# Attention over 3327 nodes on one core: query blocks of 512 instead of 476, with the remainders of two groups in one block

## The chip, the cores and the metric

The kernel runs on one core of a Trainium2 chip. The metric is the device time in microseconds (us); lower is better. Three runs of the kernel before gave a median of 9959.76 us (9959.03 to 9964.47). The profile shows one execution of the same kernel.

## The reference, cut to what matters

Two graph layers over N = 3327 nodes of 128 features. The first is a small graph attention with softmax over neighbours. The second is the expensive one: for each of d = 128 "heads" it forms a full N x N score matrix from only 8 values per node, adds the adjacency matrix twice, takes a softmax over all N keys, and multiplies with 8 values per key.

```
q = (x @ Wq.T).reshape(d, n, h)          # d = 128, n = 3327, h = 8
k = (x @ Wk.T).reshape(d, n, h)
v = (x @ Wv.T).reshape(d, n, h)
a = jnp.einsum('dnh,dmh->dnm', q, k) * scale
a = a + spatial_encoding + edge_encoding # both are the 0/1 adjacency matrix
a = jax.nn.softmax(a, axis=2)
out = jnp.einsum('dnm,dmh->dnh', a, v)
out = out.reshape(n, h * d) @ Wo.T
x = _layernorm(x + out)
```

That is 128 x 3327 x 3327, or 1.4 billion, exponentials, and as many additions or multiplications for the adjacency.

## The kernel before, in words

**Tiles.** Scores are laid out with keys in the partitions and queries along the free axis. The 3327 keys make 26 tiles of 127 or 128 keys. The 128 heads are taken in 32 groups of four (`HG = 4`, `NG = 32`). Within a group the queries are cut into `NBLK = 7` blocks: six of `WB = 476` and one of 472 (`exact`, lines 101 and 102). So there are 32 x 7 = 224 blocks, each of 26 key tiles by four heads by 476 queries.

**Per key tile.** `pair_scores` (the matmul of line 152) computes the scores of one head from 32 rows: the four heads of a group lie in the four row groups of TensorE, so they can run together. Two heads share a PSUM tile `scb` of two banks. The adjacency enters in one of two ways:

- "times": ScalarE takes the exponential of two heads from PSUM to SBUF (line 1194), then GpSimd multiplies by a factor of 1 or e squared per pair of nodes (line 1195). The factor is made once per block position by `make_factor` and kept in DRAM (`ftd`).
- "adds": VectorE adds the adjacency while it moves two heads from PSUM to SBUF (line 1197). One step later ScalarE takes the exponential of all four heads in place (line 1004, `exp_late`).

`plans` says which key tile goes which way, so that all engines are loaded: of three key tiles one is multiplied and two are added. An even-numbered and an odd-numbered block have slightly different plans. `laid` turns a plan into 26 rounds (`NR`); the rounds hold 18 or 17 exponentials of line 1194, and on average 17.5 of each kind.

**Products.** `products` (line 961) multiplies the finished exponentials `e4` with the values `v4`, which have nine columns (eight values and a one, whose sum is the softmax's divisor) in a 32-column slot. The four heads use the four column groups of TensorE, and all accumulate into one PSUM bank `av`, in the order head 0, 1, 2, 3. A product of this kind in float32 is two weight loads and two matmuls in the profile. `LAG` holds the products about five rounds behind the scores. After the last key tile, VectorE copies `av` to `o4` (line 971), which goes to DRAM (`oT`).

**Loads.** `want_adj` loads adjacency and factors three stretches ahead on SP's queue, `open_queries` the next block's queries, `open_group` the keys and values of the next group. A group is opened `OPEN` = 18 rounds before its first block, and `finish_to` forces whatever rows of the first layer it needs that are not yet done.

**Side work.** Everything else is threaded through these rounds by hand: the first layer's rows (`layer0`), their projections to q, k and v (`project`, `high`, `low`, `values`), the counts that check the input's form, and the output rows (`result`). `lane(kind, n, odd)` says in which rounds a unit of side work may go: "p" and "q" are matmuls, "d" and "l" VectorE, "m" GpSimd. Split values `hi` and `lo` (lines 396 to 425) gather 512 columns before they are stored.

**Order.** The program orders every engine's instructions by hand (`manual_schedule`); the loops of lines 1149 to 1209 write them: group, block, round.

Of the kernel before, what the change touches and what calls it, by code (L numbers as in the profile page):

```python
# [47 lines left out]
def kernel(  # L48
# [52 lines left out]
    LW = -(-(N - (NBLK - 1) * WB) // 2) * 2  # L101
    exact = [(b * WB, 0, WB) for b in range(NBLK - 1)] + [(N - LW, (NBLK - 1) * WB - N + LW, LW)]

# [20 lines left out]
    ftd = [dram.tile([NP, P, WB], F32, name=f"ftd{b}") for b in range(NBLK)]  # L124
# [25 lines left out]
    def special():  # L150
# [9 lines left out]
        with ExitStack() as sx, tc.manual_schedule(engines=ALL):  # L160
# [30 lines left out]

            ones = keep.tile([P, 1], F32, name="ones")
# [74 lines left out]
            def layer0(t, side=True, trow=None, bank=bank, held=None):  # L267
# [128 lines left out]
                def high(c, scale):  # L396
                    if c % 512 == 0:
                        s["hi"] = bg2.tile([P, 512], F32R, name="hi")
                        s["lo"] = bg2.tile([P, 512], F32R, name="lo")
                    o, hi = c % 512, s["hi"]  # L400
                    if side:
                        nc.vector.tensor_scalar(hi[:r, o : o + QW], s["b"][:r, :QW], scale, None, op0=ALU.mult)  # L402
                    else:
                        nc.scalar.mul(hi[:r, o : o + QW], s["b"][:r, :QW], scale)

                def low(dst, c, scale):
                    o = c % 512
                    hi, lo = s["hi"], s["lo"]
                    nc.vector.scalar_tensor_tensor(  # L409
                        lo[:r, o : o + QW], s["b"][:r, :QW], scale, hi[:r, o : o + QW].bitcast(F32),  # L410
                        op0=ALU.mult, op1=ALU.subtract,
                    )
                    if o + QW == 512:
                        h0 = c // 512 * 4
                        for half, sb in ((0, hi), (1, lo)):
                            at = (h0 * 2 + half if dst is qT else half * H + h0) * G + t * P * D
                            for p0, p1 in _cut(r):
                                later = held.append if held is not None and dst is qT else issue
                                engine = nc.sync if later is issue else nc.scalar
                                later(  # L420
                                    lambda at=at, sb=sb, p0=p0, p1=p1, engine=engine: engine.dma_start(
                                        _ap(dst, at + p0 * D, [[D, p1 - p0], [2 * G if dst is qT else G, 4], [1, D]]),
                                        sb[p0:p1].bitcast(F32).rearrange("p (h c) -> p h c", c=D),
                                    )
                                )

# [304 lines left out]
            def open_queries(g, b):  # L731
                q4 = qp.tile([P, WB], F32R, name="q4b")
                n0, _, w = exact[b]

                def head(j, engine=nc.sync):
                    for again in range(2):
                        engine.dma_start(
                            q4[32 * j + 16 * again : 32 * j + 16 * again + 16, :w].bitcast(F32),
                            _ap(qT, (g * HG + j) * N + n0, [[G, 2 * H], [1, w]]),
                        )  # L740

                return q4, head


            def kind(g, b):

                return (g * NBLK + b) % 2

            stretches = [
                (g, b, m) for g in range(NG) for b in range(NBLK) for m in range(len(plans[kind(g, b)]))  # L750
            ]
# [3 lines left out]
            def want_adj(n):  # L755
# [3 lines left out]
                g, b, m = stretches[n]  # L759
                a = adjs[n] = ap_.tile([P, 3, WB], F32, name="at")  # L760
                n0, _, w = exact[b]
                times, adds = plans[kind(g, b)][m]
# [26 lines left out]
            def make_factor(n):  # L789
                if n < len(stretches):  # L790
                    g, b, m = stretches[n]
                    times, _ = plans[kind(g, b)][m]
# [11 lines left out]
            with ExitStack() as st:  # L804
# [21 lines left out]
                first = layer0(0, side=False, trow=t0, bank=next_bank, held=held)  # L826
# [128 lines left out]
            def products(s, i):  # L955
                if s.left == NT:
                    s.av = pv.tile([P, WB], F32, name="av")
                r, e = kr[i], s.e.pop(i)
                s.left -= 1
                for j in range(HG):  # L960
                    nc.tensor.matmul(  # L961
                        s.av[32 * j : 32 * j + 32, : s.w],
                        s.v4[:r, j, i * H1 : i * H1 + 32],
                        e[:r, j, : s.w],
                        start=(s.left == NT - 1),
                        stop=(s.left == 0),
                    )
                if s.left == 0:
                    o4 = op_.tile([P, WB], F32, name="o4")
                    n0, c0, w = exact[s.b]  # L970
                    nc.vector.tensor_copy(o4[:, :w], s.av[:, :w])  # L971
                    for j in range(HG):
                        d = s.g * HG + j
                        issue(
                            lambda engine=nc.sync, j=j, d=d: engine.dma_start(
                                oT[:, d * N + n0 + c0 : d * N + n0 + w], o4[32 * j : 32 * j + H1, c0:w]
                            )
                        )
# [20 lines left out]
            def exp_late(now):  # L999
                for item in [x for x in late if x[0] <= now]:  # L1000
                    late.remove(item)
                    _, s, i, h0, h1 = item
                    e = s.e[i][: kr[i], h0:h1, : s.w]
                    nc.scalar.activation(e, e, AF.Exp, scale=2.0)  # L1004
# [6 lines left out]
            total = NBLK * NR  # L1011

            OPEN = min(18, total // 2)
# [6 lines left out]
            def lane(kind, n, odd):  # L1020

                n -= odd
                if n == NR - 2 and odd:
                    return int(kind != "l")
# [4 lines left out]
                return int(n % 3 == {"q": 0, "l": 2}.get(kind, 1) or n % 3 == 1 and kind == "q")  # L1029
# [25 lines left out]
            results = [((needs[t] + 1) * total + LAG + 6, result(t)) for t in range(NT - 1)]  # L1055
# [5 lines left out]
            def head(row, now, force=False):  # L1061

                while True:
                    if not side[row]:
                        if row != "main":
                            return None
                        ahead = ("rows", reads[min(max(now, 0) // total + 2, NG - 1)]) in marks
# [26 lines left out]
            def work_tensor(now, n, odd):  # L1094

                kind = head("main", now)
                if kind in ("p", "q") and lane(kind, n, odd) and side["read"] != now - 1:
                    run("main", now)

            def work(now, n, odd):  # L1100
                room, low, pool = lane("d", n, odd), lane("l", n, odd), lane("m", n, odd)
# [28 lines left out]
            queries = open_queries(0, 0)  # L1130
# [18 lines left out]
            for g in range(NG):  # L1149
                k4, v4, _ = group  # L1150
                for b in range(NBLK):
                    s = Block()
                    s.g, s.b, s.q4, s.k4, s.v4, s.left, s.e, added = g, b, queries[0], k4, v4, NT, {}, {}
                    w = s.w = exact[b][2]
                    odd = kind(g, b)
                    rounds, order, starts = plan_of[odd]
                    for n, rnd in enumerate(rounds):
                        at = b * NR + n
                        if n in starts:
                            m = number[g, b, starts[n]]  # L1160
                            if m:
                                want_adj(m + AHEAD)
                            a = adjs[m]
                        tick()
                        if n % 5 == 4 and first_loads:
                            first_loads.pop(0)[1]()
                        if g + 1 < NG:
                            if at == total - OPEN:
                                finish_to(("rows", reads[g + 1]), None)
                                tick(True)  # L1170
                                group = open_group(g + 1)
                            for k, f in enumerate(group[2]):
                                if at >= total - OPEN and at == total - OPEN + OPEN * k // len(group[2]):
                                    f()
                        if n == NR // 2 and (b + 1 < NBLK or g + 1 < NG):
                            queries = open_queries(g, b + 1) if b + 1 < NBLK else open_queries(g + 1, 0)
                        for j in range(HG):
                            if n == NR // 2 + j * (NR > 12) and (b + 1 < NBLK or g + 1 < NG):
                                queries[1](j)
                        sc = {}  # L1180
# [415 lines left out]
```

## Time and profile before

| | us |
| --- | --- |
| median of three runs | 9959.76 |
| profiled execution, whole | 9959.44 |
| its span, first to last instruction | 9957.7 |
| first exponential of line 1194 | 54.2 |
| start of the last exponential of line 1004 | 9931.2 |

The granted TensorE clock averaged 0.996 of full speed. The DMA engines were busy for some 60% of the time and moved 1755.28 MB, 176 GB/s on average.

A line of the costliest groups reads: line of the code, engine, operation, tile written and tiles read, partitions x elements, count; then busy time in total, mean nanoseconds of one; then the idle time of the engine just before such instructions, and what ended most of it. In the waits, the columns are total time, number of waits and the longest. In a timeline, they are start, duration, engine, line, operation and count. Instructions on one engine overlap: a duration runs from the start of an instruction until it is done, while the next one may start before that.

### The profile page before, as it was taken

Reading aid. Unit: us, or ns where it says so; the run is one execution under the profiler, and the core shown is the slowest. Engines: PE = TensorE matmul, PEld = TensorE weight load, DVE = VectorE, ACT = ScalarE, POOL = GpSimd, SP = SyncE. Lnnn points to the kernel's source line nnn. Section 1 sums busy time; section 2 is a strip of 40 time slices with the busy share of each in tenths; the row PEclk is TensorE's granted clock in tenths of the full one; section 3 lists DMA queues with packets and bytes.
Section 4 is the critical chain, followed back from the end, with each engine's and each line's share of the span. In section 5 each row is a group of like instructions: output and inputs, shape, how many; then the busy total and the mean of one; then the engine's idle time right before and its main releaser. Section 6 shows DMA issues by size and latency. Waiting matters only on the chain.

```text
span 9957.7 us, 207593 instructions
## 1 busy us (share of the span) xinstructions
PE 9447.6 (95%) x79523; PEld 3001.3 (30%) x79523; DVE 9210.8 (92%) x10585; ACT 9859.0 (99%) x7904; POOL 9158.9 (92%) x4923
## 2 busy tenths in 40 slices
PE   8999999999999999999999999999999999999998
PEld 3233233333233333333233333333333232222222
DVE  8999999999999999999999999999999998888888
ACT  7999999999999999999999999999999999999998
POOL 7999999999899999999999999999999998888887
PEclk9999999999999999999999999999999999999999
DMA  6666556656665656656556566566665665555554
GB/s 202 206 184 181 180 172 183 183 170 185 175 180 171 183 169 186 188 168 181 177 174 186 173 182 178 170 180 181 185 180 168 178 175 164 164 157 168 164 166 133
DMA packets 1399670, 1755.28 MB, mean 176 GB/s; under 512 B 349488, under 2 KB 1387018, under 8 KB 1394568
## 3 DMA queue, kind: packets, MB, share of 16 engines
q1 hardware_dynamic: 1395328, 1740.03, 59.4%
q8 instruction: 626, 10.26, 0.4%
q14 instruction: 380, 3.11, 0.1%
q10 hardware_dynamic: 3336, 1.88, 0.1%
HBM read 1637.49 MB, written 103.93 MB: 175 GB/s over the span
## 4 chain that ended last, share of the span: by engine, by line
ACT 44%; PE 30%; issue 10%; POOL 8%; DVE 5%; DMA 1%; SPq 0%; POOLq 0%; DVEq 0%; ACTq 0%
ACT e L1004 32%; PE av L961 15%; PE scb L152 12%; ACT e L1194 12%; POOL e L1195 7%; DVE e L1197 4%; PE bank L241 2%; DVE o L971 1%; DMA at<-in_adjT_dram 0%; POOL w L308 0%; POOL w L317 0%; DMA at<-ftd 0%; DVE dump L326 0%; DVE lo L409 0%; DMA q4b<-qT 0%
## 5 line engine op out<-in xcount | busy, mean ns | idle before, releaser
L1195 POOL TENSOR_TENSOR e<-e,at 128x952 f32<-128x952 f32 (+1 forms) x3920 | 8719.1, 2240 | 745.5 <-ACT e L1194 683.3
L1197 DVE TENSOR_TENSOR e<-scb,at 128x952 f32<-128x952 f32 (+1 forms) x7728 | 8497.2, 1141 | 681.8 <-PE scb L152 488.8
L1004 ACT ACTIVATE e<-e 128x1904 f32<-128x1904 f32 (+3 forms) x3920 | 7477.3, 1908 | 12.2 <-DVE e L1197 11.5
L961 PE MATMUL av<-e,v4b 128*32 128x476 f32 (+1 forms) x46592 | 5817.5, 572 | 44.1 <-DVE o L971 35.5
L1194 ACT ACTIVATE e<-scb 128x952 f32<-128x952 f32 (+1 forms) x3920 | 4300.2, 1097 | 35.7 <-PE scb L152 18.0
L152 PE MATMUL scb<-q4b,k4b 32*128 32x476 f32 (+1 forms) x23296 | 3861.7, 485 | 431.8 <-ACT e L1194 295.9
L152 PEld LDWEIGHTS scb<-q4b,k4b 32*128 32x128 f32 (+1 forms) x23296 | 1750.7, 189 | 5410.9 <-ACT e L1194 3210.5
L961 PEld LDWEIGHTS av<-e,v4b 128*32 128x32 f32 (+1 forms) x46592 | 1031.9, 108 | 1206.1 <-issue 1018.3
L241 PE MATMUL bank<-hsb,w 128*32 128x129 f32 (+1 forms) x5200 | 278.2, 286 | 0.0
L326 DVE TENSOR_SCALAR_CACHE_REDUCE dump<-a 128x384 bf16<-128x384 f32 (+2 forms) x468 | 247.0, 528 | 0.6
L308 POOL TENSOR_SCALAR w<-trow,er 128x129 f32<-128x129 f32 x650 | 233.8, 386 | 1.1
L317 POOL TENSOR_TENSOR w<-w,a 128x384 f32<-128x384 f32 (+3 forms) x225 | 210.1, 934 | 0.1
L241 PEld LDWEIGHTS bank<-hsb,w 128*32 128x32 f32 (+1 forms) x5200 | 102.4, 108 | 148.3 <-issue 148.3
L971 DVE COPY o<-av 128x476 f32<-128x476 f32 (+1 forms) x224 | 143.8, 642 | 3.4 <-PE av L961 3.4
L241 PE MATMUL bank<-wo,ot 128*32 128x128 f32 x1600 | 85.2, 285 | 0.0
L409 DVE SCALAR_TENSOR_TENSOR lo<-bank,hi 128x256 fp32r<-128x256 f32 (+1 forms) x200 | 82.6, 413 | 0.0
L402 DVE TENSOR_SCALAR hi<-bank 128x256 fp32r<-128x256 f32 (+1 forms) x200 | 82.4, 412 | 0.0
L241 PE MATMUL bank<-wk,x1T 128*32 128x256 f32 x800 | 63.9, 391 | 0.0
L241 PE MATMUL bank<-wv,x1T 128*32 128x256 f32 x800 | 63.9, 391 | 0.0
L241 PE MATMUL bank<-wq,x1T 128*32 128x256 f32 x800 | 63.9, 391 | 0.0
L503 PE MATMUL bank<-ident,o 128*128 128x128 f32 x225 | 52.0, 304 | 0.0
L241 PEld LDWEIGHTS bank<-wo,ot 128*32 128x32 f32 x1600 | 31.5, 108 | 45.6 <-issue 45.6
(124 smaller groups left out, 636.4 us busy)
## 6 DMA issues: line engine op xcount, KB each, us to landing
at<-in_adjT_dram SPq DMA_DIRECT2D x1536, 476.0 KB
at<-ftd SPq DMA_DIRECT2D x1674, 238.0 KB
at<-in_adjT_dram SPq DMA_DIRECT2D x256, 472.0 KB
at<-ftd SPq DMA_DIRECT2D x279, 236.0 KB
k4b<-kT SPq DMA_DIRECT2D x124, 415.9 KB
q4b<-qT SPq DMA_DIRECT2D x1536, 29.8 KB
at<-in_adjT_dram SPq DMA_DIRECT2D x192, 208.2 KB
at<-in_adjT_dram SPq DMA_DIRECT2D x150, 238.0 KB
```

Of the source, the lines that this page charges most:

```text
L152: nc.tensor.matmul(dst, k4[32 * j : 32 * j + H4, first_key(i) : first_key(i) + 2 * r - 1 : 2], q4[32 * j : 32 * j + H4, :nb], start=True, ...
L241: nc.tensor.matmul(dst[c0:c1], w[:, c0:c1], mov, **kw)
L308: nc.gpsimd.tensor_scalar(w, s["t"][:, :, :T3], -LOWEST, e, op0=ALU.min, op1=ALU.max)
L317: nc.gpsimd.tensor_tensor(w, w, s["a"][n][:, c0 - i0 : c1 - i0, :r], op=ALU.mult)
L326: nc.vector.tensor_scalar(z, a, float(k), None, op0=ALU.is_equal, op1=ALU.add, accum_out=even[:, t, at : at + 1])
L409: nc.vector.scalar_tensor_tensor(lo[:r, o : o + QW], s["b"][:r, :QW], scale, hi[:r, o : o + QW].bitcast(F32), op0=ALU.mult, op1=ALU.subtract,)
L961: nc.tensor.matmul(s.av[32 * j : 32 * j + 32, : s.w], s.v4[:r, j, i * H1 : i * H1 + 32], e[:r, j, : s.w], start=(s.left == NT - 1), stop=( ...
L971: nc.vector.tensor_copy(o4[:, :w], s.av[:, :w])
L1004: nc.scalar.activation(e, e, AF.Exp, scale=2.0)
L1194: nc.scalar.activation(eh, z[:r, :, :w], AF.Exp, scale=2.0)
L1195: nc.gpsimd.tensor_tensor(eh, eh, ah, op=ALU.mult)
L1197: nc.vector.tensor_tensor(eh, z[:r, :, :w], ah, op=ALU.add)
```

## The change

Blocks become 512 queries wide. 3327 = 6 x 512 + 255, so a group has six full blocks and a remainder of 256 (one query is computed twice). The remainders of two neighbouring groups are put side by side in one block of 512: its first half belongs to the even group, its second half to the odd one. A pair of groups thus has 13 blocks (six, the shared one, six), and the whole 208 instead of 224. In a shared block each score matmul and each product is split into two of 256 columns, since the two halves have different keys and values; exponentials, additions and multiplications cover both halves in one instruction. The adjacency of the remainder is loaded once for two groups.

Around this:

- [...] a shared block first writes zeros with one product against `nought`, and then only accumulates.
- A group whose first block comes early is opened earlier: `begins` holds the round at which a group starts (an odd group in the shared block), and group 1 is opened 10 rounds ahead, not 18.
- `lane` lets no side matmuls into shared blocks, gives "q" every round from the sixth on instead of two of three, and gives VectorE's "d" a further round of three until group 1 has begun.
- `hi` and `lo` become tiles of one projection's width (256 columns in side work), each stored on its own; the prologue gets four of them from a pool of its own.

```diff
-    LW = -(-(N - (NBLK - 1) * WB) // 2) * 2
-    exact = [(b * WB, 0, WB) for b in range(NBLK - 1)] + [(N - LW, (NBLK - 1) * WB - N + LW, LW)]
+    W = 512
+    NF = N // W
+    HALF = -(-(N - NF * W) // 2) * 2
+    exact = [(b * W, 0, W) for b in range(NF)] + [(N - HALF, NF * W - N + HALF, HALF)]
...
+            sequence = []
+            for g in range(0, NG, 2):
+                sequence += [([g], b) for b in range(NF)] + [([g, g + 1], NF)] + [([g + 1], b) for b in range(NF)]
...
+                if s.left == NT - 1 and len(s.v4) > 1:
+                    for j in range(HG):
+                        nc.tensor.matmul(s.av[32 * j : 32 * j + 32, :], nought[:r], e[:r, j, :], start=True, stop=False)
                 for j in range(HG):
-                    nc.tensor.matmul(
-                        s.av[32 * j : 32 * j + 32, : s.w],
-                        s.v4[:r, j, i * H1 : i * H1 + 32],
-                        e[:r, j, : s.w],
-                        start=(s.left == NT - 1),
-                        stop=(s.left == 0),
-                    )
+                    for k, v4 in enumerate(s.v4):
+                        nc.tensor.matmul(
+                            s.av[32 * j : 32 * j + 32, k * w : k * w + w],
+                            v4[:r, j, i * H1 : i * H1 + 32],
+                            e[:r, j, k * w : k * w + w],
+                            start=(s.left == NT - 1 and len(s.v4) == 1),
+                            stop=(s.left == 0 and k + 1 == len(s.v4)),
+                        )
...
-            OPEN = min(18, total // 2)
+            begins = [(g // 2 * 13 + g % 2 * NF) * NR for g in range(NG)]
+            OPEN = [0, 10] + [18] * (NG - 2)
...
-            def lane(kind, n, odd):
+            def lane(kind, n, odd, both):
+                if both and kind in "pq":
+                    return 0
                 n -= odd
+                if kind == "d" and opening == 1 and n > 6 and n % 3 == 2:
+                    return 1
...
-                return int(n % 3 == {"q": 0, "l": 2}.get(kind, 1) or n % 3 == 1 and kind == "q")
+                return int(kind == "q" or n % 3 == (2 if kind == "l" else 1))
...
+                        for k, k4 in enumerate(s.k4):
+                            c = slice(k * w, k * w + w)
                             for t in range(2):
-                                pair_scores(sc[i, h][: kr[i], t, :w], s.k4, s.q4, i, kr[i], 2 * h + t, w)
+                                pair_scores(sc[i, h][: kr[i], t, c], k4, s.q4[:, c], i, kr[i], 2 * h + t, w)
...
-                            ah = a[:r, at_ or 0, :w].unsqueeze(1).to_broadcast([r, 2, w])
+                        ah = a[:r, at_ or 0, :w].unsqueeze(1).to_broadcast([r, W // w * 2, w])
```

## The prediction

> **What bounds the kernel now.** I read the engine shares first, then the costliest groups, then the waits, then ScalarE's timeline start by start.
>
> ```profile
> PE 9447.6 (95%) x79523; PEld 3001.3 (30%) x79523; DVE 9210.8 (92%) x10585; ACT 9859.0 (99%) x7904; POOL 9158.9 (92%) x4923
> ...
> L1195 POOL TENSOR_TENSOR e<-e,at 128x952 f32<-128x952 f32 (+1 forms) x3920 | 8719.1, 2240 | 745.5 <-ACT e L1194 683.3
> L1197 DVE TENSOR_TENSOR e<-scb,at 128x952 f32<-128x952 f32 (+1 forms) x7728 | 8497.2, 1141 | 681.8 <-PE scb L152 488.8
> L1004 ACT ACTIVATE e<-e 128x1904 f32<-128x1904 f32 (+3 forms) x3920 | 7477.3, 1908 | 12.2 <-DVE e L1197 11.5
> ...
> L1194 ACT ACTIVATE e<-scb 128x952 f32<-128x952 f32 (+1 forms) x3920 | 4300.2, 1097 | 35.7 <-PE scb L152 18.0
> ```
>
> ScalarE is busy 99% of the span, and its two exponentials stood idle 12.2 and 35.7 us in all. VectorE and GpSimd have 7 to 8% free. The waits say the same from the other side:
>
> ```profile
> PEld scb L152 <- ACT e L1194: 3210.5, 3587, 1.5
> ...
> POOL e L1195 <- ACT e L1194: 683.3, 2284, 7.1
> ...
> ACT e L1194 <- PE scb L152: 18.0, 14, 4.0
> ...
> ACT e L1004 <- DVE e L1197: 11.5, 15, 3.1
> ```
>
> The others wait for ScalarE (TensorE 3,587 times); ScalarE waits 14 and 15 times. So ScalarE's time per instruction, start to start, is what a change must alter:
>
> ```profile
> 5014.39 1.08 ACT L1194 ACTIVATE e<-scb 128x952 f32<-128x952 f32 x1
> 5015.23 1.92 ACT L1004 ACTIVATE e<-e 128x1904 f32<-128x1904 f32 x1
> 5016.91 1.08 ACT L1194 ACTIVATE e<-scb 128x952 f32<-128x952 f32 x1
> ...
> 5093.80 1.07 ACT L1004 ACTIVATE e<-e 128x952 f32<-128x952 f32 x1
> 5094.69 1.03 ACT L1194 ACTIVATE e<-scb 128x952 f32<-128x952 f32 x1
> ```
>
> The second number, a duration, contains queueing; the differences of the first do not. L1194 over 952 elements holds the engine 0.84 us, L1004 over 1904 holds it 1.68, L1004 over 952 holds it 0.89. Medians of these differences over the whole trace: 0.843 (L1194, 952), 0.837 (L1194, 944), 1.681 (L1004, 1904), 1.668 (L1004, 1888), 0.889 (L1004, 952). From the two sizes of L1004: (1681 - 889) / 952 = 0.832 ns per element. What is left over is the fixed part: 1681 - 1904 x 0.833 = 95 ns for L1004, 843 - 952 x 0.833 = 49 ns for L1194.
>
> [...]
>
> **The change, part by part.**
>
> *Fewer, wider instructions (removed: 16 of 224 blocks).* The columns stay the same: 6 x 476 + 472 = 3328 per group before, 6 x 512 + 256 = 3328 after. So ScalarE's elements stay, and only fixed parts go. A block has 17.5 L1194 and 17.5 L1004 on average (3920 / 224), so 16 x 17.5 = 280 of each go: 280 x (95 + 49) = 40.3 us. Summed the other way, before: 3360 x 0.843 + 560 x 0.837 + 3264 x 1.681 + 544 x 1.668 + 96 x 0.889 + 16 x 0.882 = 9794.8 us. After, from 0.833 ns per element: 3640 x 0.903 + 3536 x 1.801 + 104 x 0.949 = 9753.9 us. Difference 40.9. All of it is on the path, as ScalarE never rests.
>
> *Cover by the other engines.* Before, ScalarE's first and last exponential lie at 54.2 and 9929 us: 9874.5 / 224 = 44.1 us per block. After: about 9834 / 208 = 47.3 us. GpSimd, sloped by its rows (384 elements 969 ns, 952 elements 2242 ns: 2.24 ns each): 2.40 us per instruction, 17.5 of them are 42.0 us of 47.3, 89% as before (39.2 of 44.1). VectorE: 1141 + 72 x 1.1 = 1220 ns, 34.5 of them are 42.1 of 47.3 (before 39.4 of 44.1). The side work for the rows (projections, counts, results) is unchanged in amount, 6.9% more per block, over blocks 7.3% longer. In program order no row comes too late for its group: the tightest is row 1, done at round 144 where group 1 opens at 146 (before: 153 and 164), so no burst of forced work is added. The extra slot for VectorE in the first six blocks moves its work earlier: at worst I allow 5 us once.
>
> *TensorE in an ordinary block.* A round (26 per block) is four score matmuls and four products of two matmuls each (46592 = 2 x 23296). Where nothing holds it, the timeline shows 0.43 us from scores to products and 0.93 from products to scores: 1.36 us, 35.4 of 44.1 us. Scaled by 512/476: 1.46 us, 38.0 of 47.3. Cover is kept.
>
> *TensorE in a paired block (added: 16 of them).* Same columns, twice the matmuls, of 256. Small matmuls cost more: in the side work's products of 128 columns a column group's two matmuls start 134 ns apart, of which 107 are streaming (the product sets below take 0.396 us per matmul of 476 columns, 0.83 ns per column), so about 27 ns each. Two more per group in the products and one in the scores: 1.46 + 0.08 = 1.54 us, 40 of 47.3 us. The zero product adds about 0.85 us once per block. Side work on TensorE is shut out there and moves to its neighbours. So nothing on the path, if the four column groups still run together. That is the open cost: the program now gives one group four matmuls in a row before the next group gets its first. In the trace it gives two in a row, and they do not hold the next group up:
>
> ```profile
> 9928.31 0.16 PEld L961 LDWEIGHTS av<-e,v4b 128*32 128x32 f32 x8 [0.23 <-issue]
> 9928.74 0.13 PEld L961 LDWEIGHTS av<-e,v4b 128*32 128x32 f32 x4 [0.27 <-issue]
> 9929.13 0.13 PEld L961 LDWEIGHTS av<-e,v4b 128*32 128x32 f32 x4 [0.27 <-issue]
> ```
>
> Eight loads start within 0.16 us, the next four only when the first matmuls end, 0.4 us later, and each product set takes 0.79 us: four groups at once. With four in a row, bounds are 0 and a halving (two groups at a time): 0.85 us more a round. I take 0, since a matmul waiting for its own group did not stop the others.
>
> *DMA and SP.* Adjacency and factor columns fall from 32 x 3328 to 32 x 3200, -3.8%; query and output transfers keep their number (192 x 8 + 16 x 16 = 1792 query loads); key and query stores of the side work double in number at half the size. SP mostly waits for adjacency buffers (2694 us for VectorE, 1433 for GpSimd), and ScalarE waits for DMAs about 11 us in all: no gain, no loss.
>
> *Ends.* The last block is 512 wide instead of 472: its six last product sets (4.98 us of loads and matmuls back to back) grow by 0.4 us, the copy and the transfer by 0.2. The prologue's four split buffers instead of two can save the 2 us that it waits for stores, or nothing; I take nothing.
>
> *Sum.* 9957.7 - 40.9 + 0.6 = 9917.4 us of span; the profiled execution is 1.7 us above its span (9959.44), so 9919 us. That execution lies 0.3 us under the median of the runs (9959.76). ScalarE's remaining stalls stay as they are: 83 us above the medians, 31 of them before 400 us.
>
> **The rivals.**
>
> *Paired blocks leak a little.* Pipeline refills at each change of block shape, or a partly lost overlap, cost 1 to 2.5 us in each of 16 blocks: 16 to 40 us back, 9935 to 9959, about 9945. For it: GpSimd and VectorE have only 11% of slack, and scores of two key tiles must be fetched before ScalarE gets its next bank. Against: TensorE waits 3,210 us for ScalarE, 0.8 us per exponential.
>
> *Column groups run two at a time in paired blocks (slower than before).* A round then takes 1.46 + 0.85 = 2.31 us, a block 60 us against 47.3, and 16 blocks lose 13 us each: 9919 + 206 = 10125. It decides once a round loses more than 1.82 - 1.54 = 0.28 us; with groups each held up by one matmul (3 x 0.213 = 0.64 us) it is 26 x 0.36 x 16 = 150 us, 10069. For it: [...] only one waiting matmul per group is seen. Against: the loads above.
>
> *Wider instructions do not save the fixed part*, because ScalarE's cost goes by rows of 476 rather than by instruction: then 9957. Against it: two rows of L1004 take 0.889 us and four take 1.681, which leaves 97 ns once, not per row.
>
> **How the numbers follow.** Measurement tells about 0.2% (20 us) from no change. ScalarE stays full: 70%, 9919 with its own range 9907 to 9935. Paired blocks leak: 14%, a third of it still more than 20 us faster. Fixed part not saved: 3%. Column groups in series: 13%. Range 9905 to 9958 leaves out the last case and the outer edges of the others, about 18%. Faster 0.74, same 0.13, slower 0.13.
>
> **What would show it.** ScalarE's start-to-start steps should be 0.90 us after an exponential from PSUM and 1.80 us after a full one in SBUF, 3640 instructions of each kind; TensorE's clock stays granted at 1.00. In paired blocks, the loads of all four groups should begin within some 0.2 us and a block should last 47 us; if such blocks last 55 to 60 us with ScalarE idle behind the scores, the slower rival holds. If ScalarE's step for 1024 elements is above 0.92 us, the per-instruction saving is wrong.

## The result, and the profile after

The changed kernel takes 9924.86 us (median of 7 runs, 9920.19 to 9930.75), the kernel before 9959.54 us beside it (7 runs). The ratio is 0.9965, 95% interval 0.9953 to 0.9976: about 35 us faster. In the profiled execution the span is 9918.3 us, against 9957.7 before.

The page of the kernel after, the engines and the costliest groups (in its code, L1227 is what L1194 was, L1016 what L1004 was):

```profile
PE 9233.4 (93%) x79651; PEld 2974.5 (30%) x79651; DVE 9147.4 (92%) x10018; ACT 9814.5 (99%) x7344; POOL 9115.2 (92%) x4643
...
L1228 POOL TENSOR_TENSOR e<-e,at 128x1024 f32<-128x1024 f32 x3640 | 8672.8, 2397 | 748.6 <-ACT e L1227 694.6
L1230 DVE TENSOR_TENSOR e<-scb,at 128x1024 f32<-128x1024 f32 (+1 forms) x7176 | 8436.0, 1217 | 705.3 <-PE scb L155 551.5
L1016 ACT ACTIVATE e<-e 128x2048 f32<-128x2048 f32 (+2 forms) x3640 | 7592.5, 2086 | 15.3 <-DVE e L1230 14.7
...
L1227 ACT ACTIVATE e<-scb 128x1024 f32<-128x1024 f32 x3640 | 4427.2, 1216 | 38.0 <-PE scb L155 25.1
```

ScalarE is the bound as before: 99% busy, its two exponentials idle for 15.3 and 38.0 us (12.2 and 35.7 before). GpSimd takes 2397 ns per instruction and VectorE 1217 (worked out ahead: 2.40 us and 1220 ns), with the same shares of the span. What has changed is ScalarE's step. Its timeline, start, duration, engine, line:

```profile
5011.91 2.12 ACT L1016 ACTIVATE e<-e 128x2048 f32<-128x2048 f32 x1
5013.71 1.24 ACT L1227 ACTIVATE e<-scb 128x1024 f32<-128x1024 f32 x1
5014.61 2.14 ACT L1016 ACTIVATE e<-e 128x2048 f32<-128x2048 f32 x1
```

The starts are 1.80 and 0.90 us apart. The medians over the trace are 1.802 us (2048 elements), 0.903 (1024 from PSUM) and 0.950 (1024 in SBUF). Over all steps, ScalarE's sum (the median step of each form, times its count) is 9756.6 us, against 9795.2 before: 38.6 us less. What it waits above that sum is 81.2 us, against 81.9: the same in total, but not the same waits, as the experiments show. This accounts for the span, which is 39.4 us shorter: 38.6 from the steps, 0.7 from the waits, 1.0 from a first exponential at 53.2 us instead of 54.2, less 0.9 at the end.

### The profile page after: what moved, and what is told of

Its sections match the earlier page's. It is cut to its first block, busy times and chain, and to the rows that moved or that the text cites. A ratio compares the mean times of both kernels' runs of the same rounds, so it can differ in the third digit from the quotient of the medians.

```text
span 9918.3 us, 205530 instructions
## 1 busy us (share of the span) xinstructions
PE 9233.4 (93%) x79651; PEld 2974.5 (30%) x79651; DVE 9147.4 (92%) x10018; ACT 9814.5 (99%) x7344; POOL 9115.2 (92%) x4643
## 3 DMA queue, kind: packets, MB, share of 16 engines
q10 hardware_dynamic: 3336, 1.89, 0.1%
## 4 chain that ended last, share of the span: by engine, by line
ACT 52%; PE 20%; issue 11%; POOL 7%; DVE 5%; DMA 1%; SPq 0%; POOLq 0%; DVEq 0%; ACTq 0%
ACT e L1016 36%; ACT e L1227 15%; PE scb L155 9%; PE av L972 9%; POOL e L1228 7%; DVE e L1230 3%; PE bank L246 2%; DVE o L982 1%; POOL w L313 0%; DMA at<-in_adjT_dram 0%; POOL w L322 0%; DMA at<-ftd 0%; PE av L969 0%; DVE dump L331 0%; PE bank L506 0%
## 5 line engine op out<-in xcount | busy, mean ns | idle before, releaser
L1228 POOL TENSOR_TENSOR e<-e,at 128x1024 f32<-128x1024 f32 x3640 | 8672.8, 2397 | 748.6 <-ACT e L1227 694.6
L1230 DVE TENSOR_TENSOR e<-scb,at 128x1024 f32<-128x1024 f32 (+1 forms) x7176 | 8436.0, 1217 | 705.3 <-PE scb L155 551.5
L1016 ACT ACTIVATE e<-e 128x2048 f32<-128x2048 f32 (+2 forms) x3640 | 7592.5, 2086 | 15.3 <-DVE e L1230 14.7
L972 PE MATMUL av<-e,v4b 128*32 128x512 f32 (+2 forms) x46592 | 5738.6, 571 | 39.1 <-DVE o L982 26.5
L1227 ACT ACTIVATE e<-scb 128x1024 f32<-128x1024 f32 x3640 | 4427.2, 1216 | 38.0 <-PE scb L155 25.1
L155 PE MATMUL scb<-q4b,k4b 32*128 32x512 f32 (+2 forms) x23296 | 3664.7, 476 | 608.4 <-ACT e L1227 499.2
L155 PEld LDWEIGHTS scb<-q4b,k4b 32*128 32x128 f32 (+1 forms) x23296 | 1653.1, 189 | 5397.0 <-ACT e L1227 3387.3
L972 PEld LDWEIGHTS av<-e,v4b 128*32 128x32 f32 (+1 forms) x46592 | 1101.9, 108 | 1181.4 <-issue 890.3
L982 DVE COPY o<-av 128x512 f32<-128x512 f32 x208 | 141.3, 680 | 4.1 <-PE av L972 4.0
```

The lines of the kernel that those rows point to most:

```text
L155: nc.tensor.matmul(dst, k4[32 * j : 32 * j + H4, first_key(i) : first_key(i) + 2 * r - 1 : 2], q4[32 * j : 32 * j + H4, :nb], start=True, ...
L972: nc.tensor.matmul(s.av[32 * j : 32 * j + 32, k * w : k * w + w], v4[:r, j, i * H1 : i * H1 + 32], e[:r, j, k * w : k * w + w], start=(s.l ...
L982: nc.vector.tensor_copy(o4, s.av)
L1227: nc.scalar.activation(eh, z, AF.Exp, scale=2.0)
L1228: nc.gpsimd.tensor_tensor(eh, eh, ah, op=ALU.mult)
L1230: nc.vector.tensor_tensor(eh, z, ah, op=ALU.add)
```

## The experiments

Eight kernels ran in two sets, each set beside its own runs of the kernel before. The first set (the yardstick, the zero product, the order of the products, the early opening) is compared with the changed kernel of the same set. The second has no run of the changed kernel, and its kernel before took 9963.84 us, 4 to 5 us more than the others; so where it is set against the changed kernel's 9925, the difference is uncertain by as much.

**The yardstick.** No edit.

> The changed kernel once more, as the yardstick for the three beside it. All theories: about 35 us below the kernel before, a span near 9918 us, ScalarE's steps 0.903 us (1024 elements from PSUM) and 1.802 us (2048 in SBUF).

Measured: 9923.97 us (median of 5), ratio 0.9963 (0.9950 to 0.9977); the profiled span is 9922.3 us. So two profiles of one kernel differ by 4 us. Nearly half of it lies ahead of the first exponential, which starts at 53.2 us in one and 55.0 in the other. What ScalarE waits above its sum is 87.5 us here, against 81.2 in the first profile.

**What the fixed part is: exponentials in SBUF, split.** In the changed kernel:

```diff
-                    nc.scalar.activation(e, e, AF.Exp, scale=2.0)
+                    for c in range(0, h1 - h0, 2):
+                        nc.scalar.activation(e[:, c : c + 2], e[:, c : c + 2], AF.Exp, scale=2.0)
```

> In the changed kernel, each full exponential in SBUF (2048 elements, four heads) is done as two of 1024 (two heads each): 3536 instructions more, the same elements. Theory (ScalarE pays 95 ns per such instruction): 3536 x 95 ns = 336 us more, about 10260, with steps of 0.95 us. Rival (ScalarE pays per row or per element only): no change, about 9924.

Measured: 10228.05 us in one run, 303 above the changed kernel's 9925. ScalarE's timeline (a row "x2" holds two instructions):

```profile
5009.97 2.37 ACT L1017 ACTIVATE e<-e 128x1024 f32<-128x1024 f32 x2
5011.86 1.38 ACT L1228 ACTIVATE e<-scb 128x1024 f32<-128x1024 f32 x1
5012.77 2.37 ACT L1017 ACTIVATE e<-e 128x1024 f32<-128x1024 f32 x2
```

Two halves hold the engine for 1.89 us where the whole held it for 1.80. The medians: 0.947 for a half, so 2 x 947 - 1802 = 92 ns for one instruction more, 325 us for 3536 of them. ScalarE's waits fell to 60 us from 84 (the mean of the two profiles of the changed kernel), as the others had more time: 325 - 24 = 301, close to the measured 303. The cost, 92 ns, is per instruction. That it goes by rows or elements alone is excluded, since both are as before.

**The same for exponentials from PSUM.** In the changed kernel:

```diff
-                            nc.scalar.activation(eh, z, AF.Exp, scale=2.0)
+                            half = eh.shape[1] // 2
+                            for c in (0, half):
+                                nc.scalar.activation(eh[:, c : c + half], z[:, c : c + half], AF.Exp, scale=2.0)
```

> In the changed kernel, each exponential from PSUM (1024 elements, two heads) is done as two of 512 (one head each): 3640 instructions more. Theory (49 ns per instruction that reads PSUM): 178 us more, about 10102, steps of 0.476 us. Rival (the 49 ns belong to the change from SBUF to PSUM, and a neighbour of the same kind costs 95): up to 346 us more, about 10270. Rival per row: no change.

Measured: 10135.21 us in one run, 210 more. ScalarE's timeline:

```profile
5012.32 1.38 ACT L1229 ACTIVATE e<-scb 128x512 f32<-128x512 f32 x2
5013.27 2.22 ACT L1016 ACTIVATE e<-e 128x2048 f32<-128x2048 f32 x1
```

Two halves hold the engine for 0.95 us where the whole held it for 0.90. The median step of a half is 0.477 us, whether an instruction of the same kind or one in SBUF follows; two of them cost 954 against 903, 51 ns more, 186 us in all. The other 24 us are waits (98 us against 84), the 104 exponentials over 1024 elements in SBUF, whose step grew from 0.950 to 1.054 us (11 us), and the start (55.8 us against 53.2 to 55.0). So the smaller fixed part (51 ns) goes with reading PSUM, not with the alternation.

**Width without pairing.** In the kernel before, blocks of 512 and the remainder of 256 as a block of its own, 224 blocks as before:

```diff
-    WB = -(-N // (2 * NBLK)) * 2
+    WB = 512
...
-            op_ = sx.enter_context(tc.tile_pool(name="sx_o", bufs=2))
+            op_ = sx.enter_context(tc.tile_pool(name="sx_o", bufs=1))
```

> The kernel before with blocks of 512 and the last 256 queries of each group in a block of their own: again 224 blocks and 3920 exponentials of each kind (one buffer for the copied products instead of two, to make room). Theory (only the number of instructions matters, not the width): ScalarE's own sum is that of the kernel before, 9795 us, so at least 9955; in the short blocks VectorE (34.5 instructions of about 0.68 us, 23.6 us, with its side work 26) exceeds ScalarE's 25.0 us, so up to 3 us more in each of 32 blocks, 9960 to 10060. Rival (the width itself gains): 9920 to 9940.

Measured: 10293.86 us (median of 4), ratio 1.0333 (1.0315 to 1.0350). The total alone could hide a gain of the width under the loss, but ScalarE's steps show none: 0.903 and 1.801 us, as in the changed kernel. With 0.477 and 0.950 us for the two short forms, the instructions of this run add to 9796 us, no less than in the kernel before. But the loss was far beyond the range given, and where it lies is not where I put it. The windows of three blocks in a row, ordinary, short and ordinary (columns: stretch, its length, busy time and count of PE, PEld, DVE, ACT, POOL, then granted clock, DMA share, GB/s):

```profile
4774.20:4822.10 47.90, 45.28 (x391) 14.29 (x393) 44.59 (x53) 47.90 (x36) 42.15 (x19) 1.00 0.45 134
4822.10:4853.70 31.60, 30.61 (x378) 13.35 (x370) 24.87 (x46) 27.78 (x37) 24.43 (x20) 1.00 0.74 160
4853.70:4904.50 50.80, 47.53 (x400) 15.22 (x400) 44.05 (x42) 47.73 (x36) 44.37 (x29) 0.90 0.54 174
```

The short block lasts 31.6 us where ScalarE alone needs 25, and TensorE is busy for 30.6 of it; VectorE, which I had named, for 24.9. TensorE's weight loads, for scores and products in turn, start 0.57 to 0.65 us apart in most of the stretch below, and of their 27 waits ahead of the scores in this block, 14 (5.8 us) are for nothing that the profile shows ("issue"):

```profile
4834.72 0.52 PEld L152 LDWEIGHTS scb<-q4b,k4b 32*128 32x128 f32 x4 [0.41 <-issue]
4835.36 0.16 PEld L961 LDWEIGHTS av<-e,v4b 128*32 128x32 f32 x8
4835.93 0.52 PEld L152 LDWEIGHTS scb<-q4b,k4b 32*128 32x128 f32 x4 [0.41 <-issue]
4836.58 0.16 PEld L961 LDWEIGHTS av<-e,v4b 128*32 128x32 f32 x8
4837.15 0.20 PEld L152 LDWEIGHTS scb<-q4b,k4b 32*128 32x128 f32 x4 [0.41 <-ACT e L1194]
...
4838.05 0.51 PEld L152 LDWEIGHTS scb<-q4b,k4b 32*128 32x128 f32 x4 [0.41 <-issue]
```

Two rounds of three take 1.21 to 1.22 us here and the third 0.90 (from one load for the scores to the next), 1.11 on average without side work, where ScalarE's 25 us leave 0.96 for each of 26. So TensorE is the likely bound in these blocks, though over the one shown its loads also waited 5.0 us for ScalarE. They last 31.6 us on average.

The blocks after a short one take 51.7 us on average instead of 46.1 to 48.0. What happens first there can be read from the trace (columns as above):

```profile
4852.40:4855.80 3.40, 1.40 (x16) 0.50 (x12) 1.43 (x2) 1.78 (x2) 0.96 (x1) 0.99 0.92 225
4855.80:4866.00 10.20, 10.04 (x58) 2.56 (x58) 8.41 (x8) 8.39 (x7) 7.12 (x3) 0.50 0.95 336
```

VectorE waits 2.4 us for adjacency and TensorE 2.3 us for VectorE. Then the granted clock reads 0.50 for 10.2 us, and TensorE is busy throughout. The same is seen in all 29 such blocks after 1000 us: the clock reads half for 6.8 to 30.7 us (in three of them from within the short block on), and TensorE was busy for only 15 to 85% of the 3.4 us before that. Of the 141 us that ScalarE loses in these blocks, 120 fall while the clock reads half or within 1.5 us after. Whether the late transfers bring the idle time, and the idle time the low clock, no run tried.

Over the whole trace ScalarE waits 384 us above its own medians, against 82; the medians of the short forms (0.494 and 0.980 us) already hold some waiting. The single buffer for the copied products has little part in it: VectorE's copies waited 10 us in all, nearly all of it for TensorE. Laying two remainders side by side keeps ScalarE's instructions large, and it also spares such blocks: shared blocks last 46.8 to 48.8 us (below).

**The zero product.** In the changed kernel, the first product of a shared block starts the bank with its first half only; the second half's product then adds, without a start of its own:

```diff
-                if s.left == NT - 1 and len(s.v4) > 1:
-                    for j in range(HG):
-                        nc.tensor.matmul(s.av[32 * j : 32 * j + 32, :], nought[:r], e[:r, j, :], start=True, stop=False)
...
-                            start=(s.left == NT - 1 and len(s.v4) == 1),
+                            start=(s.left == NT - 1 and k == 0),
```

> The product with zeros at the start of each shared block is gone; the first half's product starts the bank, the second half's adds to it. Theory (the zero product delays the scores that ScalarE needs next, about 0.75 us in each of 16 blocks): 12 us less than the changed kernel, and a shared block lasts as long as an ordinary one. Rival (the loss comes from the change of matmul size itself): no change, shared blocks still 0.75 us longer.

The reason to try it was this stretch of the changed kernel's timeline, early in a shared block:

```profile
2830.40 0.75 PEld L155 LDWEIGHTS scb<-q4b,k4b 32*128 32x128 f32 x8 [0.84 <-issue]
...
2831.44 0.16 PEld L969 LDWEIGHTS av<-e,nought 128*32 128x32 f32 x8 [0.28 <-DVE o L982]
...
2833.34 0.33 PEld L155 LDWEIGHTS scb<-q4b,k4b 32*128 32x128 f32 x8 [0.41 <-issue]
...
2833.97 1.03 ACT L1227 ACTIVATE e<-scb 128x1024 f32<-128x1024 f32 x1 [0.56 <-PE scb L155]
```

The zero product waits for VectorE's copy of the last block, then runs ahead of the real products, and the next scores are loaded only at 2833.34. The exponential that needs them starts 0.9 us late (2.70 us after the L1016 before it, instead of 1.80). The same place without the zero product:

```profile
2828.80 2.15 ACT L1011 ACTIVATE e<-e 128x2048 f32<-128x2048 f32 x1
...
2830.01 0.42 PEld L155 LDWEIGHTS scb<-q4b,k4b 32*128 32x128 f32 x8 [0.41 <-issue]
...
2830.64 1.22 ACT L1222 ACTIVATE e<-scb 128x1024 f32<-128x1024 f32 x1
```

The exponential now starts 1.84 us after the one before it. Measured: 9910.24 us (median of 5), ratio to the kernel before 0.9951 (0.9937 to 0.9964), 13.7 us below the yardstick, and the two ranges do not overlap. In the trace the shared blocks last 47.95 and 46.01 us (medians of even and odd ones) instead of 48.77 and 46.77, just as ordinary ones do (47.96 and 46.10). Outside the first shared block, which lies in the busy start, ScalarE's waits in shared blocks fall from 13.2 and 13.9 us (two profiles of the changed kernel) to 0.9: 12 to 13 us, as expected. This version is the fastest that ran, and it shows that the zero product was not needed; that it was needed was an assumption of the change, which no trace had shown.

**Order of the products in a shared block.** In the changed kernel:

```diff
-                for j in range(HG):
-                    for k, v4 in enumerate(s.v4):
+                for k, v4 in enumerate(s.v4):
+                    for j in range(HG):
```

> In a shared block the products go half by half, the four column groups in turn inside each half, instead of four matmuls in a row for one group. Theory (the column groups run together either way): the time of the changed kernel within 3 us, products of a shared round 1.0 us as there. Rival (four in a row hold the other groups up in part): products of a shared round shorter by 0.1 us or more, and the time lower by up to 10 us.

Measured: 9925.47 us (median of 5), 1.5 above the yardstick, with ranges that overlap (9920.65 to 9928.97 against 9918.45 to 9925.36). The 16 matmuls of one round's products start in four sets of four, in both kernels, though the changed kernel gives all four of one group in a row: within a set they start 13 ns apart there, 7 ns here. From the first to the last start it is 692 ns (median), against 712 in the changed kernel. So four matmuls in a row for one column group hold the others up by 20 ns. The weight loads in such a block, first of the changed kernel, then of this run:

```profile
2835.05 0.33 PEld L155 LDWEIGHTS scb<-q4b,k4b 32*128 32x128 f32 x8 [0.64 <-ACT e L1227]
2835.51 0.61 PEld L972 LDWEIGHTS av<-e,v4b 128*32 128x32 f32 x16
2836.53 0.73 PEld L155 LDWEIGHTS scb<-q4b,k4b 32*128 32x128 f32 x8 [0.41 <-issue]
```

```profile
2836.02 0.32 PEld L155 LDWEIGHTS scb<-q4b,k4b 32*128 32x128 f32 x8 [0.67 <-ACT e L1227]
2836.47 0.59 PEld L972 LDWEIGHTS av<-e,v4b 128*32 128x32 f32 x16
2837.47 0.76 PEld L155 LDWEIGHTS scb<-q4b,k4b 32*128 32x128 f32 x8 [0.41 <-issue]
```

All 16 loads are done within 0.61 us, and a round takes 1.48 us (2835.05 to 2836.53) in the changed kernel and 1.45 here, of the 1.82 that ScalarE leaves.

**The early opening of a group.** The zero product left out, and in addition the extra VectorE slot of the first blocks:

```diff
-            OPEN = [0, 10] + [18] * (NG - 2)
+            OPEN = [0, 5, 14] + [18] * (NG - 3)
...
-                if kind == "d" and opening == 1 and n > 6 and n % 3 == 2:
-                    return 1
```

> Without the zero product, and without the extra slot for VectorE in the first six blocks: group 1 is opened 5 rounds ahead instead of 10 and group 2 14 instead of 18, so that the rows are ready without it. Theory (the extra slot made ScalarE wait some 7 us more for VectorE and the scores between 100 and 420 us): 7 us below the kernel without the zero product, 19 below the changed kernel. Rival (the early waits come from the transfers and the lower TensorE clock of the start): the same as without the zero product, or slower, since the keys of group 1 arrive late.

Measured: 9911.23 us (median of 5), 1.0 above the version without the zero product, within the spread of both: no gain, where 7 us were expected. The waits of ScalarE between 90 and 420 us (time, number, longest), first of the kernel without the zero product, then of this one:

```profile
ACT e L1011 <- DVE e L1225: 12.1, 22, 1.6
ACT e L1222 <- PE scb L155: 10.0, 13, 2.0
```

```profile
ACT e L1220 <- PE scb L155: 13.4, 10, 5.0
ACT e L1011 <- DVE e L1223: 7.0, 11, 1.3
```

The waits for VectorE did fall by 5.1 us, but those for scores rose by 3.4, with one of 5.0 us among them. In the same stretch, TensorE's scores waited 5.0 us for the keys from DRAM, which they did not in the other kernel. So the late opening takes back much of what leaving out the slot gains; as both were changed in one run, what the slot alone costs was not measured.

**Stores of the split values, alone.** In the kernel before, only `hi` and `lo` as in the change, with four buffers in the prologue:

```diff
-                    if c % 512 == 0:
-                        s["hi"] = bg2.tile([P, 512], F32R, name="hi")
-                        s["lo"] = bg2.tile([P, 512], F32R, name="lo")
-                    o, hi = c % 512, s["hi"]
+                    s["hi"] = pool.tile([P, QW], F32R, name="hi")
+                    s["lo"] = pool.tile([P, QW], F32R, name="lo")
```

> The kernel before with one part of the change alone: the split values stored per 256 columns, twice as many stores of half the size, and four buffers for them in the prologue. Theory: no change within 3 us (0 to 2 less from the prologue). Rival (this side change carries part of the gain): 5 to 15 us less.

Measured: 9970.02 us (median of 12) against 9963.84, ratio 1.0008 (0.9999 to 1.0016). It carries none of the gain. It is 6 us slower, more than the 3 us allowed for; by the interval its cost is between none and 0.16%. The first exponential starts at 54.17 us, as before (54.16), so the prologue gained nothing.

## Why the prediction was right

- *ScalarE's fixed part.* Predicted 40.9 us less, measured 38.6 in the sums of medians (the steps are 1.802 and 0.903 us against 1.801 and 0.903); one nanosecond in the longer step is 3.5 us, and the yardstick's profile, which reads 1.801, gives 42.0. The two splits measure the terms by themselves: 92 and 51 ns where 95 and 49 were used.
- *Cover by GpSimd, VectorE and the side work.* It held. Their shares of the span are as before, and ScalarE's waits are the same in total within what two profiles differ by (81.2 and 87.5 us, against 81.9).
- *TensorE in a shared block.* Predicted 1.54 us a round, measured 1.48, and the four column groups run together (four starts within 40 ns). The slower rival, priced at 10069 to 10125 us, is refuted by the loads and by the changed order (20 ns).
- *The zero product.* It "adds about 0.85 us once per block", and "nothing on the path" was the prediction for the shared block. The second part was wrong: it cost 12 to 13 us over the shared blocks without the first, by the run without it. Its length was right (about 0.9 us in the trace, from its loads to those of the first real products), but its place is in front of the scores that ScalarE waits for. The rival of leaking shared blocks (16 to 40 us) named the place but not this cause.
- *The start.* Between 100 and 400 us ScalarE's waits grew from 21 to 28 us. The prediction allowed 5 us at worst for the extra slot and put nothing into its sum; how much of the 7 us is the slot's stays open.
- *Why the sum still fits.* By luck, as far as the waits go. These two losses add to some 20 us that the sum did not have, and yet the total of the waits hardly moved. After 1000 us they were 49 us before, and are 39 in one profile of the changed kernel and 45 in the other, with the shared blocks' loss among them; so they fell elsewhere by 18 to 22 us. Part of it can be placed: around three stretches of 3.4 us in which the granted clock read half, at 4794, 5146 and 8348 us, ScalarE lost 9 us before; the changed kernel has one such stretch in one profile and two in the other, with 1 and 4 us. Much of the rest fell at the change from block to block (at the fourth exponential of a block, 8.4 us before and 2.7 after), and why was not tried. The predicted span, 9917.4 us, lies 0.9 from the profiled 9918.3, closer than two profiles of one kernel (9918.3 and 9922.3), and that profile was of the fastest of seven runs. The predicted 9919 us lies just below all seven, 5.9 us (0.06%) from their median.

## What to carry to other kernels

When one engine is busy without a gap, price a change by its start-to-start steps at two sizes: their slope and rest say what fewer, larger instructions save (here 40.9 us predicted, 38.6 measured), and splitting one instruction in two confirms it (92 and 51 ns here, for 95 and 49 from the steps). A narrow remainder is worth pairing with another, since the saving counted by instruction here (9796 us for ScalarE's instructions with as many of them as before, 9756.6 with fewer), and TensorE did not get through the narrow block in proportion (it was busy for 30.6 us in a block of 256 queries and for 45.3 in one of 512). Small work that is put once at the head of a block was not free here, since what stood behind it in TensorE's order was awaited: the zero product, about 0.9 us long, cost 12 to 13 us over the shared blocks. Look at what such work is queued in front of, not only at the engine's slack.

## What the runs showed of the hardware that was not expected

The fixed part of an exponential depends on its source: 49 to 51 ns from PSUM, 92 to 95 from SBUF, on top of 0.83 ns per element. For matmuls on four column groups, handing four in a row to one group costs 20 ns of 712, so a group that waits for itself holds back the others by no more than that. After a start on the first half of a bank, the second half's first product needed no zeros ahead of it, by the run that leaves them out (9910.24 us, against 9923.97 with them). In the run of unpaired blocks, the granted TensorE clock read half for 6.8 to 30.7 us around the start of the block after a short one, in all 29 such blocks after 1000 us, each time after 3.4 us in which TensorE was busy for 15 to 85%, though it had been busy for 30.6 of 31.6 us in the short block shown. The mean over that run was 0.976, where all other profiles of whole kernels had 0.995 to 0.997. In the kernel before, the three half-clock stretches after 1000 us also followed 3.4 us in which TensorE was busy for 39 to 58%. What the clock goes by was not tried.
